# h and u in the weights' column order, and three q pairs turned by VectorE from quarter rows

## The chip, the cores and the metric

The kernel runs on one core of a Trainium2 chip. Five engines work at the same time, each through its own queue in order: TensorE (PE, with its weight loads shown apart as PEld), VectorE (DVE), ScalarE (ACT), GpSimd (POOL) and SyncE (SP). DMA transfers are issued from the queues of SP, ACT and POOL. The metric is the time of one execution on the device in microseconds (us); lower is better.

## What is computed

One layer of attention over a sparse graph, with a layer norm before it and a residual behind it. There are N = 2708 nodes with D = 1024 features, all float32. A row of `adj` has about four ones.

```python
h = jnp.maximum(_layernorm(x, axis=-1), 0.0)
q = h @ W_q.T + b_q
k = h @ W_k.T + b_k
v = h @ W_v.T + b_v
z = scale * (q @ k.T) * adj
z = jnp.where(z == 0.0, -10000.0, z)
attn = jax.nn.softmax(z, axis=1)
out = x + jax.nn.relu(attn @ v)
```

## The kernel before

**The algebra.** The kernel doesn't form k and v. It forms M = scale * W_q^T W_k once, then for each node the row q = h M + b, the scores z as products of q with the rows h of the node's neighbours, u as the softmax-weighted sum of those same rows, and the output as relu(u W_v + b_v) + x. The neighbours' rows are gathered from `h_dram` in HBM by indirect DMAs.

**Tiles.** The nodes are sorted by their number of neighbours into 22 tiles of 128 rows (the last one is small). A tile of rows lies in SBUF as 128 partitions of 1024 columns.

**The order of columns.** The weights come from HBM with their 1024 columns in the order "p c": feature c * 128 + p stands at column p * 8 + c. A slice of W_q for one c therefore takes every eighth column (`a_tile`, L464). Before the change h, q and u lie in natural order, "c p". The product that makes M comes out of PE in the weights' order, so `evicted` (L489) and `joined` (L492) permute its columns while they copy it from PSUM to SBUF, and so does the copy of the bias at L596.

**Units.** From about 106 us on, the work of PE is a sequence of 20 units, each a pair of tiles: ten q pairs (tiles 0 to 19) and ten o pairs (u times W_v). A unit multiplies 256 rows by a 1024x1024 matrix in seven block products instead of eight, with sums and differences of blocks (`multiply`, L1044, `opened`, L1015, `add_block`, L1008). Each block product is eight records of PE of 128x512, written to the banks `ps` or `psy`. The right-hand blocks are M and T (T is built by `ts_of_m`, L438, and lies in `wlow`).

**Turning the rows.** The left-hand blocks need features on the partitions, so each pair of tiles has to be turned. `blocks` (L711) makes, for a pair (xa, xb), the turned halves a11, a12 (of xa), a22 and a21 (of xb), and from these s1 = a22 + a21, s3 = a11 - a21, s2 = s1 - a11 and s4 = a12 - s2. There are two ways of turning. In `half_turned` (L410) PE turns 128x128 squares against an identity: the square is PE's stationary operand, four turns go into one PSUM bank, and ScalarE copies the bank to SBUF (L718). The q pairs go this way, and two single u tiles that are kept in SBUF. In `faces` (L703) VectorE turns 32x32 squares with one instruction for half a tile (L705); that only gives the wanted result if the rows were laid out by quarters first, and `by_quarters` (L695) does that with four DMAs from SP when u is read back from `u_dram`. For that, ScalarE first copies u into a tile v with the columns of a quarter side by side (L944) and stores v. The o pairs go this way.

**Where the rows of a q pair come from.** Units 0 to 3 (tiles 0 to 7) use the tiles that the layer norm left in SBUF. Units 4 to 9 gather their rows of h from HBM on POOL (`load_rows`, L1198, `gather`, L607) once the table of sorted rows is back in SBUF.

**What sets the order.** In unit n the function `after(i)` (L1245) runs between the products: it asks for the turning of pair n + 1 (upper half at i = 0, lower half at i = 2, in a few units later), for the rows of pair n + 2, and advances the stream of scores (L863) and sums (L923) on VectorE by an amount of work for each step. ScalarE and VectorE follow a fixed order up to unit 4, VectorE up to the end; POOL follows one up to unit 2 and is then ordered by the scheduler. Before the units, `stats`, `root`, `apply` (L270) and `keep` (L278) make h: `apply` writes relu of the normed x over x. POOL adds each tile into `hsum` (L285, L298). The positions `pos_i` for the sort of tiles 0 to 7 are made at (3, 6), that is unit 3, step 6; POOL then scatters the table (`put`, L622, written at L626), it is loaded back, and the gathers for the scores (L610) begin.

## Time and profile before

| what | value |
|---|---|
| median of 3 runs | 635.86 us (634.95 to 635.87) |
| the profiled execution | 631.83 us |
| its span in the profile | 630.1 us |
| instructions | 6067 |
| DMA moved | 182.19 MB |

The profile shows one execution. Its stages are: products of the weights up to about 104 us; q units from 106 to about 350 us; o units up to about 605 us; a single last tile up to 624 us. In a row of the profile, L1010 is line 1010 of the kernel, `out<-in,in` gives tiles by the program's names, `x8` is a count, and what stands in brackets is idle time of the engine before the row with what ended it. A group's row ends in busy us, mean ns of one, and idle us before. Records of PE overlap, because a product is still draining when the next one begins; the distance between starts is what one costs.

The kernel's line that a row names is one before the change. Of the rows used below, L415 is a turn on PE, L476 a product of the weights, L1010 a product of a unit, L705 a half turn on VectorE, L722 the making of s1 to s4, L863 a score, L923 a sum.

### The profile page before, as it was taken

The page shows a single profiled execution, that of the slowest core. Times are in us where ns is not written, and L with a number is a line of the kernel's source. Part 1 is how long each engine was busy: PE and PEld are TensorE (multiplying, and loading weights), DVE is VectorE, ACT ScalarE, POOL GpSimd, SP SyncE. Part 2 cuts the span into 40 slices and gives each one's busy share as a digit, 9 for nine tenths or more (in the row PEclk, how much of TensorE's full clock was granted, in tenths as well). Part 3 has the DMA queues.
Part 4 walks back from the last instruction along what each step waited for, and adds up shares of the span by engine and source line. Part 5 has one row for each costly group of instructions (what it writes and reads, how often), then busy time and mean ns, then how long its engine had stood idle before and what let it go on. Part 6 is the DMA issues. An engine that isn't in the chain of part 4 may idle for free.

```text
span 630.1 us, 6067 instructions
## 1 busy us (share of the span) xinstructions
PE 619.6 (98%) x1579; PEld 310.3 (49%) x1579; DVE 523.3 (83%) x1022; ACT 288.4 (46%) x421; POOL 363.1 (58%) x394
## 2 busy tenths in 40 slices
PE   8999999999999999999999998999999999999996
PEld 5777766444444444454454443444444444444442
DVE  5999879997996664887988969999997999988741
ACT  3538985749677563343341333434342323343300
POOL 2649860885778177754561632757667477852241
PEclk9999999999999999999999999999999999999999
DMA  8999997688796439997489998899999999997481
GB/s 330 407 371 326 343 354 294 209 288 326 255 387 241 166 113 319 350 379 236 154 306 325 332 359 265 235 333 346 347 318 324 344 278 305 349 284 194 103 296 71
DMA packets 65088, 182.19 MB, mean 289 GB/s; under 512 B 9959, under 2 KB 20023, under 8 KB 64408
## 3 DMA queue, kind: packets, MB, share of 16 engines
q0 software_dynamic: 26656, 86.02, 43.4%
q1 hardware_dynamic: 31594, 71.53, 32.8%
q10 hardware_dynamic: 6798, 24.20, 9.8%
q8 instruction: 14, 0.23, 0.2%
q14 instruction: 26, 0.21, 0.1%
HBM read 146.70 MB, written 43.36 MB: 302 GB/s over the span
## 4 chain that ended last, share of the span: by engine, by line
PE 56%; DMA 17%; DVE 11%; issue 9%; POOL 4%; ACT 1%; SPq 1%; POOLq 0%; DVEq 0%; ACTq 0%
PE ps L1010 22%; PE psy L1010 15%; PE ps_y L476 7%; DMA out_dram<-y,tab 5%; PE ps_x L476 4%; DMA or<-u_dram 4%; PE ps_z L476 4%; DVE junk L863 4%; PE pt L415 3%; DMA pq<-q_late 2%; DVE u L923 2%; DMA q_late<-q 2%; DMA g<-h_dram,tab 2%; DMA u_dram<-v 1%; DVE a L705 1%
## 5 line engine op out<-in xcount | busy, mean ns | idle before, releaser
L1010 PE MATMUL psy<-wlow,s 128*128 128x512 f32 x320 | 144.0, 592 | 0.0
L1010 PE MATMUL ps<-M,a 128*128 128x512 f32 x320 | 144.0, 593 | 0.0
L610 POOL DMA_INDIRECT g<-h_dram,tab x91 | 110.3, 1212 | 55.8 <-ACT u L912 19.8
L863 DVE SCALAR_TENSOR_TENSOR junk<-g,pq 128x1024 uint8<-128x1024 f32 x90 | 110.0, 1223 | 16.8 <-DMA g<-h_dram,tab 10.2
L1010 PE MATMUL ps<-M,s 128*128 128x512 f32 x240 | 108.0, 592 | 2.2 <-DVE s L722 2.2
L1010 PEld LDWEIGHTS psy<-wlow,s 128*128 128x128 f32 x320 | 59.9, 190 | 72.4 <-issue 70.2
L1010 PEld LDWEIGHTS ps<-M,a 128*128 128x128 f32 x320 | 59.9, 190 | 71.8 <-issue 71.3
L923 DVE SCALAR_TENSOR_TENSOR u<-g,coef,u 128x1024 f32<-128x1024 f32 x66 | 84.6, 1282 | 4.9 <-ACT u L912 3.5
L1010 PEld LDWEIGHTS ps<-M,s 128*128 128x128 f32 x240 | 45.4, 190 | 59.7 <-issue 58.3
L389 DVE FIND_INDEX8 at<-ones,adj 128x8 uint32<-128x685 f32 (+1 forms) x88 | 74.5, 865 | 0.0
L1010 PE MATMUL psy<-wlow,a 128*128 128x512 f32 x160 | 72.0, 593 | 0.1
L368 ACT ACTIVATE sized<-adj 128x2708 uint8<-128x2708 f32 (+1 forms) x22 | 54.3, 2466 | 7.5 <-DMA adj<-in_adj_dram 6.1
L298 POOL TENSOR_TENSOR hsum<-hsum,x 128x256 f32<-128x256 f32 (+1 forms) x56 | 38.7, 728 | 25.4 <-DVE wlow L444 22.0
L1109 POOL DMA_INDIRECT y<-in_x_dram,tab x19 | 32.2, 1696 | 31.4 <-ACT y L1126 22.4
L1010 PEld LDWEIGHTS psy<-wlow,a 128*128 128x128 f32 x160 | 30.3, 190 | 38.7 <-issue 37.3
L944 ACT COPY v<-u 128x1024 f32<-128x1024 f32 x19 | 19.9, 1045 | 48.9 <-DVE u L923 43.5
L808 POOL DMA_INDIRECT out_dram<-y,tab x21 | 27.8, 1325 | 22.0 <-issue 13.6
L1010 PE MATMUL ps<-wlow,s 128*128 128x512 f32 x80 | 36.0, 592 | 0.0
L626 POOL DMA_INDIRECT tab_dram<-tab,pos_i x22 | 21.9, 993 | 20.9 <-DVE pos_i L689 15.4
L912 ACT ACTIVATE u<-g,coef 128x1024 f32<-128x1024 f32 x18 | 20.7, 1148 | 24.2 <-DVE coef L911 24.1
L760 ACT COPY ps<-bp_sb 128x512 f32<-128x512 f32 x42 | 24.6, 595 | 11.0 <-DVE y L1144 10.3
L276 ACT ACTIVATE x<-x,r 128x1024 f32<-128x1024 f32 (+1 forms) x22 | 25.8, 1232 | 5.6 <-POOL r L266 5.6
(251 smaller groups left out, 848.5 us busy)
## 6 DMA issues: line engine op xcount, KB each, us to landing
adj<-in_adj_dram SPq DMA_DIRECT2D x21, 1354.0 KB, 11.2
x<-in_x_dram SPq DMA_DIRECT2D x21, 512.0 KB, 4.2
h_dram<-x ACTq DMA_DIRECT2D x21, 512.0 KB, 8.4
u_dram<-v ACTq DMA_DIRECT2D x19, 512.0 KB, 8.5
or<-u_dram SPq DMA_DIRECT2D x76, 128.0 KB, 9.7
q_late<-q SPq DMA_DIRECT2D x12, 512.0 KB, 9.4
pq<-q_late POOLq DMA_DIRECT2D x12, 512.0 KB, 10.5
M<-in_wv_dram SPq DMA_DIRECT2D x3, 1024.0 KB, 15.4
```

The lines of the kernel that those rows point to most:

```text
L276: nc.scalar.activation(xs[i][:n], xs[i][:n], AF.Relu, bias=r[:n, 4, i:i + 1], scale=r[:n, 3, i:i + 1])
L298: small.append(nc.gpsimd.tensor_add(hsum[:n, cols], hsum[:n, cols], xt[:n, cols]))
L368: nc.scalar.activation(sized[:n], a[:n, :, :PW], AF.Abs, accum_out=total[:n, t:t + 1])
L389: nc.vector.max_index(at[:n, k - first_k, g, :], ones[:n, 0:8], a[:n, g, :])
L476: mm = nc.tensor.matmul(bank, a_tile(o + H * a[0], a[1], i), b(o), start=first and o == 0, stop=(o == H - 1), skip_group_check=True)
L610: return nc.gpsimd.indirect_dma_start(out=dst, out_offset=None, in_=src, in_offset=off, bounds_check=N - 1, oob_is_err=False)
L760: nc.scalar.copy(return_[h], row[:, h * NB:(h + 1) * NB])
L808: to = nc.gpsimd.indirect_dma_start(out=out, out_offset=bass.IndirectOffsetOnAxis(ap=ptab.bitcast(U32)[:n, t, SLOTS:SLOTS + 1], axis=0), i ...
L863: chained(lambda: nc.vector.scalar_tensor_tensor(junk, g_of[t][s], 1.0, tq[t], op0=ALU.mult, op1=ALU.mult, accum_out=zall[:, t, s:s + 1]))
L923: chained(lambda: nc.vector.scalar_tensor_tensor(u, g_of[t][s], coef[:, s:s + 1], u, op0=ALU.mult, op1=ALU.add))
L1010: mm = nc.tensor.matmul(bank, a[:, c, :], b[:, c, :], start=False, stop=(c == 3), skip_group_check=True)
L1109: return nc.gpsimd.indirect_dma_start(out=y[:n], out_offset=None, in_=x, in_offset=off, compute_op=ALU.add)
```

## The change

h, q, M and u now lie in the weights' column order "p c" everywhere, and three q pairs are turned by VectorE.

- `evicted`, `joined` and the copy of the bias no longer permute; `joined` is one instruction for a bank instead of two. `ts_of_m` works on contiguous halves and its order is slightly different.
- `apply` writes h into another tile than x, with the columns permuted: each write steps over eight columns (32 bytes). For this there is one more row tile (`row_extra`), and the seven row tiles are now handed out by name.
- A turn on PE takes every eighth column of the tile as its square (`half_turned`), in place of 128 neighbouring columns.
- `faces` reads every eighth column of the laid-out tile, in place of runs of 32 neighbours.
- u is stored as it is; the copy v on ScalarE is gone.
- The q pairs of units 5, 6 and 7 (tiles 10 to 15) are gathered by quarter rows: `quarter_ids` makes an index table with 16 small operations on VectorE, and `gather_quarters` issues four indirect DMAs for a tile, 256 columns each, in place of one of 1024. These tiles go through `faces`.

```diff
     def apply(first, only=range(4)):
...
-                nc.scalar.activation(xs[i][:n], xs[i][:n], AF.Relu, bias=r[:n, 4, i:i + 1], scale=r[:n, 3, i:i + 1])
+                ht = spare.pop()
+                nc.scalar.activation(ht[:n].rearrange("p (m c) -> p c m", c=DC), xs[i][:n].rearrange("p (c m) -> p c m", c=DC),
+                                     AF.Relu, bias=r[:n, 4, i:i + 1], scale=r[:n, 3, i:i + 1])
+                spare.append(xs[i])
...
     def half_turned(xt, s):
...
-            k = s * 4 + c
-            nc.tensor.transpose(pt[:, c, :], xt[:, k * P:(k + 1) * P], ident)
+            nc.tensor.transpose(pt[:, c, :], xt.rearrange("p (m c) -> p c m", c=DC)[:, s * 4 + c], ident)
...
         def joined(bank, g, half, i):
-            for j in range(2):
-                nc.vector.scalar_tensor_tensor(place(g, half, i)[:, j], taken(bank)[:, j], scale,
-                                               place(g, half, i)[:, j], op0=ALU.mult, op1=ALU.add)
+            nc.vector.scalar_tensor_tensor(place(g, half, i), bank, scale, place(g, half, i), op0=ALU.mult, op1=ALU.add)
...
+    quartered = range(2 * FIRST + 2, 2 * FIRST + 8)
...
+        for g in range(QUADS):
+            for a in range(QUADS):
+                nc.vector.tensor_scalar(quarter_i[a * QP:(a + 1) * QP, g], ptab.bitcast(U32)[g * QP:(g + 1) * QP, lo:hi, SLOTS],
+                                        float(QUADS), float(a), op0=ALU.mult, op1=ALU.add)
+
+    def gather_quarters(dst, t):
+
+        faced.append(dst)
+        for g in range(QUADS):
+            off = bass.IndirectOffsetOnAxis(ap=quarter_i[:, g, t - quartered[0]:t - quartered[0] + 1], axis=0)
+            nc.gpsimd.indirect_dma_start(out=dst[:, g * D // QUADS:(g + 1) * D // QUADS], out_offset=None,
+                                         in_=h_dram.rearrange("n (a j) -> (n a) j", a=QUADS), in_offset=off)
...
         return nc.vector.transpose(dst.rearrange("p c (g r) -> p g c r", r=QP),
-                                   xt.rearrange("p (g c r) -> p g c r", g=QUADS, r=QP)[:, :, lo:hi])
+                                   xt.rearrange("p (g r c) -> p g c r", g=QUADS, r=QP)[:, :, lo:hi])
...
-            v = row_tile(f"v_{t}")
-            nc.scalar.copy(v.rearrange("p (a c r) -> p c a r", a=QUADS, r=QP),
-                           u.rearrange("p (c a r) -> p c a r", a=QUADS, r=QP))
-            nc.scalar.dma_start(u_dram[t * P:(t + 1) * P, :], v)
+            nc.scalar.dma_start(u_dram[t * P:(t + 1) * P, :], u)
...
-            if kind == "q":
+            if kind == "q" and t in quartered:
+                gather_quarters(rows[-1], t)
+            elif kind == "q":
                 gather(rows[-1], h_dram[:, :], t, SLOTS, P)
...
-                rows_of[FIRST + 1] = load_rows(units[FIRST + 1])
                 pooled.close()
+            if (n, i) == (3, 0):
+                quarter_ids()
+                rows_of[FIRST + 1] = load_rows(units[FIRST + 1])
```

On PE, in unit 4, between the product of a22 and that of s2 and further, the rows before are these (`qr` are the gathered rows of tiles 10 and 11, `pt` the bank of turned squares; a row with x8 is eight turns, one of x4 a block product):

```order
L1010 MATMUL psy<-wlow,a_1236 128x512 x4
L678 LDWEIGHTS before
L678 MATMUL ps_in<-sort,before 128x144
L680 LDWEIGHTS ones_h
L680 MATMUL ps_all<-sort,ones_h 128x144
L415 MATMUL pt<-ident,qr_1312 128x128 x8
L1010 MATMUL psy<-wlow,s_1434 128x512 x4
L415 MATMUL pt<-ident,qr_1314 128x128 x8
L1010 MATMUL ps_1373<-M,a_1396 128x512 x4
```

And now:

```order
L1026 MATMUL psy<-wlow,a_1220 128x512 x4
L698 LDWEIGHTS before
L698 MATMUL ps_in<-sort,before 128x144
L700 LDWEIGHTS ones_h
L700 MATMUL ps_all<-sort,ones_h 128x144
L1026 MATMUL psy<-wlow,s_1436 128x512 x4
L1026 MATMUL ps_1375<-M,a_1398 128x512 x4
```

The two rows of eight turns are gone; the same holds for the next two units.

On VectorE, in unit 5, where the first scores and the s blocks of unit 6 are made (`g` are gathered rows, `pq` the rows of q, `junk` the product that is thrown away), the rows before are:

```order
L863 SCALAR_TENSOR_TENSOR junk_1673,zall<-g_1402,pq_1611 128x1024
L863 SCALAR_TENSOR_TENSOR junk_1675,zall<-g_1403,pq_1611 128x1024
L863 SCALAR_TENSOR_TENSOR junk_1677,zall<-g_1404,pq_1611 128x1024
L722 TENSOR_TENSOR s_1691<-a_1684,pt 128x512
L722 TENSOR_TENSOR s_1693<-a_1658,pt 128x512
L722 TENSOR_TENSOR s_1695<-s_1691,a_1658 128x512
```

And now:

```order
L723 STREAM_TRANSPOSE a_1640<-row_168 128x4x4x32
L723 STREAM_TRANSPOSE a_1642<-row_168 128x4x4x32
L882 SCALAR_TENSOR_TENSOR junk_1650,zall<-g_1404,pq_1598 128x1024
L882 SCALAR_TENSOR_TENSOR junk_1652,zall<-g_1405,pq_1598 128x1024
L882 SCALAR_TENSOR_TENSOR junk_1654,zall<-g_1406,pq_1598 128x1024
L723 STREAM_TRANSPOSE a_1656<-row_169 128x4x4x32
L723 STREAM_TRANSPOSE s_1658<-row_169 128x4x4x32
L740 TENSOR_TENSOR s_1660<-a_1656,s_1658 128x512
```

Four half turns have come in, two ahead of the scores and two behind them, and s1 no longer reads a bank of PE.

On POOL, between the last additions to `hsum` and the scatter of the early table, the rows before are (`qr` again gathered rows, of tiles 10 to 13):

```order
L298 TENSOR_TENSOR hsum<-hsum,x_945 128x256 x4
L612 DMA qr_1312<-h_dram,tab 128x1024
L612 DMA qr_1314<-h_dram,tab 128x1024
L612 DMA qr_1579<-h_dram,tab 128x1024
L612 DMA qr_1581<-h_dram,tab 128x1024
L626 DMA tab_dram_70<-tab,pos_i 1024x18 x8
```

And now, with `row` for the row tiles of tiles 10 to 15:

```order
L310 TENSOR_TENSOR hsum<-hsum,row_167 128x256 x4
L634 DMA row_166<-h_dram,quarter_i 128x256 x4
L634 DMA row_167<-h_dram,quarter_i 128x256 x4
L634 DMA row_168<-h_dram,quarter_i 128x256 x4
L634 DMA row_169<-h_dram,quarter_i 128x256 x4
L634 DMA row_164<-h_dram,quarter_i 128x256 x4
L634 DMA row_165<-h_dram,quarter_i 128x256 x4
L646 DMA tab_dram_70<-tab,pos_i 1024x18 x8
```

24 indirect DMAs of 256 columns stand ahead of the scatter, where four of 1024 columns stood.

More of the change, by code (lines that the diff above doesn't have):

```diff
@@ L438, in ts_of_m @@
     def ts_of_m(part, *which):
-        cut = slice(part * (P // NH), (part + 1) * (P // NH))
-        m = [[M[:, i, j].rearrange("p c (b w) -> p (c b) w", w=P)[:, :, cut] for j in range(2)] for i in range(2)]
-        t = [T[:, k].rearrange("p c (b w) -> p (c b) w", w=P)[:, :, cut] for k in range(4)]
+        cut = slice(2 * part, 2 * part + 2)
+        m = [[M[:, i, j, cut] for j in range(2)] for i in range(2)]
+        t = [T[:, k, cut] for k in range(4)]
         for k in which:
```

59 lines of the change are left out of this document (30 added, 29 removed).

## Prediction

> **What bounds the kernel now.** I read the page first, for the busy shares, and then who waited for whom on PE.
>
> ```profile
> span 630.1 us, 6067 instructions
> PE 619.6 (98%) x1579; PEld 310.3 (49%) x1579; DVE 523.3 (83%) x1022; ACT 288.4 (46%) x421; POOL 363.1 (58%) x394
> ```
>
> ```profile
> PE ps L1010 <- DVE s L722: 2.2, 1, 2.2
> PE ps_y L511 <- POOL hsum L121: 1.2, 1, 1.2
> PE ps L1010 <- DVE T_alone L705: 0.8, 1, 0.8
> PE ps_x L476 <- DMA wlow<-in_wq_dram: 0.6, 1, 0.6
> ```
>
> PE is busy for 619.6 of 630.1 us, and all its waits add to 4.8 us. A busy PE need not be PE at its best, so I looked at the stretches: the columns are PE, PEld, DVE, ACT and POOL busy with counts, then granted clock, DMA share and GB/s.
>
> ```profile
> 35.00:107.00 72.00, 72.00 (x187) 52.38 (x187) 63.98 (x161) 52.79 (x65) 43.78 (x63) 1.00 0.92 339
> 107.00:200.00 93.00, 93.00 (x250) 43.38 (x249) 82.50 (x213) 67.56 (x82) 66.61 (x103) 1.00 0.81 290
> ...
> 240.00:330.00 90.00, 90.00 (x259) 43.39 (x258) 74.62 (x120) 33.57 (x57) 56.41 (x49) 1.00 0.84 290
> 330.00:400.00 70.00, 67.84 (x159) 29.79 (x158) 62.63 (x104) 22.75 (x37) 25.16 (x22) 1.00 0.95 305
> 400.00:600.00 200.00, 200.00 (x479) 89.30 (x478) 181.56 (x294) 73.34 (x119) 124.24 (x95) 1.00 0.95 294
> ```
>
> PE is full in every stretch shown but one, at the full granted clock of 1.00. **So each microsecond that PE's own queue gains or loses comes out at the end**, unless VectorE, 0.9 busy from 330 us on, is late instead. The chain of waits shows what the turns cost PE now:
>
> ```profile
> 138.74 0.87 PE pt L415 x8
> ```
>
> Eight turns of 128x128 take 0.87 us, 0.109 us each.
>
> **Part 1: turns taken from PE.** Three pairs leave PE, 16 turns each, 48 of the 176 that the table below counts (64, 96 and 16): 48 x 0.109 = **-5.2 us**. ScalarE loses nine copies of 0.59 us with them, and the 19 copies of u; both lie beside PE.
>
> **Part 2: the turns that stay.** 176 - 48 = 128 stay on PE. Their stationary operand was a block of 128 neighbouring columns and is now every eighth column, a step of 32 bytes. The trace has that step already: the products of the weights (L476) load wq's columns with the same step of eight. The rows of the weight load, with its mean in ns after the comma:
>
> ```profile
> L1010 PEld LDWEIGHTS ps<-M,a 128*128 128x128 f32 x320 | 59.9, 190 | 71.8 <-issue 71.3 <-ACT ps L760 0.5
> ...
> L415 PEld LDWEIGHTS pt<-ident,qr 128*128 128x128 f32 x96 | 11.2, 141 | 5.8 <-issue 5.6 <-DVE g L1262 0.2
> ...
> L476 PEld LDWEIGHTS ps_x<-wk,wq 128*128 128x128 f32 x32 | 10.0, 313 | 3.7
> ...
> L415 PEld LDWEIGHTS pt<-ident,x 128*128 128x128 f32 x64 | 7.4, 141 | 3.3 <-issue 3.2
> L415 PEld LDWEIGHTS pt<-ident,u 128*128 128x128 f32 x16 | 1.9, 141 | 1.1 <-issue 1.1
> ...
> L594 PEld LDWEIGHTS ps_v<-acc_b,ones 128*128 128x128 f32 x4 | 0.8, 190 | 0.8 <-issue 0.5 <-PE ps_y L476 0.2
> ```
>
> The same 128x128 f32 load is 190 ns with neighbouring columns, 313 with the step; L594 stands among the L476 loads in time and is 190, so the step makes the difference, not the stage. Today those 313 ns are hidden, since one L476 product takes 13.9 us / 32 = 0.43 us. A turn has only 0.109 us to hide a load. How close two loads can follow each other is seen where nothing covers them, right after a wait of PE:
>
> ```profile
> 5.70 0.55 PEld L476 LDWEIGHTS ps_x<-wlow 128*128 128x128 f32 x2 [1.04 <-DMA wlow<-in_wk_dram]
> ...
> 390.41 0.30 PEld L1010 LDWEIGHTS ps<-M,s 128*128 128x128 f32 x2 [2.96 <-issue]
> ...
> L476 PE MATMUL ps_x<-wk,wq 128*128 128x512 f32 x32 | 13.9, 592 | 0.0
> ```
>
> Two loads with the step take 0.55 us together, so the second starts 0.55 - 0.31 = 0.24 us after the first; without it 0.30 - 0.19 = 0.11. The part of a record that holds up the next load is thus its length less 0.08: 0.11 of 0.19, 0.23 of 0.31, 0.06 of 0.14. No row shows a turn with the step. Its load is bounded below by 0.06 (then nothing changes, the 0.109 of the turn covers it) and above by 0.24. I take 0.232, the nearest row: the same tile, type and step. The first load of a run hides under the product before it; in PE's order the 128 turns stand in 15 runs (one of 16, fourteen of 8), so 113 are uncovered: 113 x (0.232 - 0.109) = **+13.9 us**, with ends 0 and 113 x 0.131 = +14.8.
>
> [...]
>
> **Part 3: VectorE.** It gets 12 half turns of the three pairs, and all its half turns now read with the step of 32 bytes.
>
> ```profile
> L705 DVE STREAM_TRANSPOSE a<-or 128x512 f32<-128x512 f32 x28 | 18.6, 693 | 0.0
> ...
> L688 DVE TENSOR_REDUCE deg<-sort 128x14 f32<-128x252 f32 x1 | 0.6, 594 | 0.0
> L688 DVE TENSOR_REDUCE deg<-sort 128x8 f32<-128x144 f32 x1 | 0.4, 420 | 0.0
> L662 DVE TENSOR_REDUCE bad<-sort 128x14 f32<-128x224 f32 x1 | 0.4, 386 | 0.0
> L662 DVE TENSOR_REDUCE bad<-sort 128x8 f32<-128x128 f32 x1 | 0.3, 285 | 0.0
> ```
>
> A half turn is 0.69 us. L688 reads its 144 elements with just this step, its 252 with 56 bytes; L662 reads neighbours. Per element that is (594 - 420) / 108 = 1.61 ns against (386 - 285) / 96 = 1.05. I take 512 x 0.56 ns, **about +0.3 us for a half turn**, ends 0 and +0.4 (by 420 against 302 at 144 elements). Where it counts is where products wait for VectorE:
>
> ```profile
> 379.88 1.30 DVE L705 STREAM_TRANSPOSE a<-or 128x512 f32<-128x512 f32 x2
> ...
> 388.90 0.66 DVE L705 STREAM_TRANSPOSE s<-or 128x512 f32<-128x512 f32 x1
> 389.60 0.69 DVE L722 TENSOR_TENSOR s<-a,s 128x512 f32<-128x512 f32 x1
> ...
> 390.44 3.67 PE L1010 MATMUL ps<-M,s 128*128 128x512 f32 x8 [2.16 <-DVE s L722]
> ...
> 411.97 0.69 DVE L722 TENSOR_TENSOR s<-a,s 128x512 f32<-128x512 f32 x1
> ...
> 414.55 1.88 PE L1010 MATMUL ps<-M,s 128*128 128x512 f32 x4
> ```
>
> At 390 us PE already waits 2.16 for s1, and four half turns stand ahead of it from 379.88 on: 4 x 0.3 = **+1.3 us** with rounding up. At 414 s1 is 1.9 us early and the next four are covered. The other 28 from 400 us on add 9 us, less than the 18.4 us that VectorE is idle there.
>
> The quarter gathers meet VectorE through POOL, whose queue they enter ahead of the tables' scatter:
>
> ```profile
> 206.59 0.93 POOL L612 DMA_INDIRECT qr<-h_dram,tab  x1 [0.30 <-issue]
> 219.24 1.00 POOL L626 DMA_INDIRECT tab_dram<-tab,pos_i  x1 [11.72 <-DVE pos_i L689]
> ...
> 240.75 1.23 DVE L863 SCALAR_TENSOR_TENSOR junk<-g,pq 128x1024 uint8<-128x1024 f32 x1 [5.17 <-DMA g<-h_dram,tab]
> ...
> 248.05 1.28 DVE L722 TENSOR_TENSOR s<-a,pt 128x512 f32<-128x512 f32 x2 [3.21 <-ACT a L718]
> ...
> 260.98 3.60 PE L1010 MATMUL ps<-wlow,s 128*128 128x512 f32 x8
> ```
>
> A gather takes 0.93 us and 0.30 to the next; 24 stand there instead of 4, so 20 x 1.23 = 25 us, of which POOL's 11.72 of idle time take half. The scatter, and with it the first scores on VectorE, comes about 13 us later if PE is not delayed, and some 10 if it is (part 2 holds up the sort too). Behind those scores stands s1 of unit 6, made at 248.7 and needed at 260.98: 12.2 us of slack, and the wait of 3.21 for ScalarE's copies goes while two half turns of 1.0 come. That just covers it. VectorE must then win back its lag, up to 13.3 - 3.2 + 2.0 + 4.0 (unit 7) + 1.2 = 17.3 us, by 390 us; it has 15.4 - 5.2 - 3.2 = 7.0 idle us to 330 and 7.4 to 400, 14.4. If all of the lag comes, 2.9 us reach PE; with the 1.3 that is +4.2. The other end is -2.2, the wait at 390 gone. I keep +1.3.
>
> **Part 4: hidden.** ScalarE's 22 writes of h now step 32 bytes.
>
> ```profile
> L276 ACT ACTIVATE x<-x,r 128x1024 f32<-128x1024 f32 x21 | 24.7, 1232 | 5.6 <-POOL r L266 5.6
> ...
> L944 ACT COPY v<-u 128x1024 f32<-128x1024 f32 x19 | 19.9, 1045 | 48.9 <-DVE u L923 43.5 <-DVE u L929 5.3
> ```
>
> Even at VectorE's price for such reads (1024 x 0.82 ns) these are 18 us, in the 45 us that ScalarE is idle between 35 and 200 us; without that cover they would hold up evictions one for one. The 16 index operations lie in VectorE's 10.5 idle us before 200. Evictions without a permutation and eight joins for sixteen gain nothing, as PE waits for none of them. At the end, u's copy of 1.05 us leaves the way to T_alone and the double half turn gains 0.6: zero, within the 0.8 that PE waits there.
>
> **Sum.** -5.2 + 13.9 + 1.3 = **+10.0 us**. The profiled execution took 631.83 us (span 630.1), the runs' median is 635.86. I add the sum to the median: **645.9 us**. Its own range runs from -5.2 + 13.9 - 2.2 = +6.5 to -5.2 + 14.8 + 4.2 = +13.8: 642.4 to 649.7.
>
> **The rivals.**
> - *The step is hidden on PE: faster.* If a turn's load passes each element once where a product's passes it twice, which 0.06 against 0.11 would allow, the step makes 0.06 x 2.14 = 0.126 at most, 113 x 0.017 = +1.9 us. Then -5.2 to -3.3, about 631.6. Place: the runs of eight turns. It decides at a load of 0.144 us: below it (5.2 - 1.3) / 113 = 0.035 a turn is not used up. For it: nothing shows a turn paying. [...] Against it: 0.24 us for the same read.
> - *The step adds its 0.123 to the 0.06.* Then a load is 0.182: 113 x 0.073 = +8.2, in sum +4.3, 640.2.
> - *The step is hidden, and VectorE becomes the bound.* The lag of part 3 in full: -5.2 to -3.3, and +4.2, in the middle about 635.8, no change. For it: the 2.16 at 390.
>
> **How the numbers follow.** A measurement of this kernel can tell about 0.2%, 1.3 us. Chances: the forecast 0.50, the added step 0.13 (both slower: 0.63), VectorE as the bound 0.13 (same), the hidden step 0.24 (faster). The range of 631.5 to 649.7 leaves out the better half of the faster case and the forecast's worst.
>
> **What would show it.** Eight turns take 0.87 us in the chain if the step is free, 0.98 if hidden up to 0.126, 1.7 by the forecast; a turn's load is 0.31 long, not 0.14; half turns on VectorE are near 1.0 us; POOL's first scatter of the early table starts with no idle time before it; PE's wait for s1 near 390 us is over 3. It is wrong if the load of a turn stays under 0.15 us, or if a new wait of PE between 250 and 400 us is larger than 4.2.

## The result, and the profile after

The changed kernel takes **669.1 us** (667.91 to 670.36, four runs); the kernel before, on the same chip beside it, 635.87 us. The ratio is 1.0522, with a 95% interval from 1.0494 to 1.0551: slower by 33.2 us. The forecast was +10.0 us and its range ended at 649.7.

The head of the page of the changed kernel, beside 630.1 us, 98% PE and 523.3 us of DVE before:

```profile
span 668.3 us, 5994 instructions
...
PE 625.4 (94%) x1531; PEld 309.2 (46%) x1531; DVE 551.9 (83%) x1042; ACT 287.5 (43%) x393; POOL 382.2 (57%) x412
```

TensorE has 48 matmuls less and was still busy 5.8 us longer; its idle time went from 10.5 to 42.9 us. The waits of PE say for what (engine, tile and line waited for, then us in total, times, longest):

```profile
PE psy L1026 <- issue: 13.2, 1, 13.2
PE pt L426 <- ACT M L496: 5.7, 2, 5.3
PE psy L1026 <- DVE q L1107: 4.9, 2, 3.4
PE psy L1026 <- ACT psy L1039: 2.9, 2, 2.5
PE ps L1026 <- ACT ps L778: 2.7, 1, 2.7
PE ps L1026 <- DVE T_alone L723: 2.6, 1, 2.6
PE ps L1026 <- DVE s L740: 1.9, 1, 1.9
```

Before, the longest wait was 2.2 us. Now TensorE waits for copies on ScalarE (the evictions of L496 and L1039, and L778, which puts the bias into a bank), for VectorE (q, s, T_alone), and once for something that the profile does not show ("issue"). The stretches, with the columns of those before:

```profile
35.00:107.00 72.00, 68.79 (x161) 49.31 (x159) 58.59 (x130) 60.86 (x52) 44.61 (x62) 1.00 0.85 314
107.00:200.00 93.00, 89.20 (x252) 44.24 (x252) 80.89 (x222) 71.70 (x81) 59.15 (x92) 0.96 0.76 267
240.00:330.00 90.00, 74.86 (x181) 33.70 (x182) 61.63 (x100) 25.24 (x44) 58.31 (x62) 0.92 0.72 242
330.00:400.00 70.00, 66.49 (x163) 29.64 (x162) 65.14 (x99) 19.90 (x34) 34.92 (x28) 0.98 0.89 292
400.00:600.00 200.00, 198.07 (x471) 87.79 (x470) 191.69 (x292) 61.97 (x108) 121.46 (x96) 1.00 0.98 302
```

Every stretch has lost some of TensorE's time, the last one 1.9 us, and in the three between 107 and 400 us the granted clock is under 1.00 too. Where the time went is seen best by setting the same product of the two kernels side by side. Both run the same 140 block products on TensorE and then the last tile; the table gives how much later a product starts in the changed kernel than in the kernel before, at the places where that changes most (the two profiled executions; starts in us). Smaller steps are left out, four of about 0.67 us between 442 and 529 us among them:

```
before   after    later by  step
106.58   114.74    8.16    +8.16   first products of the blocks
190.37   201.19   10.82    +2.71
217.15   227.23   10.08    -0.87   eight turns gone; so at 221, 243, 247, 269 and 273
228.33   250.95   22.62   +13.37   the wait "issue"
231.76   256.19   24.43    +1.81   a product of 5.2 us instead of 3.4
235.19   262.45   27.26    +2.83
290.20   315.74   25.54    +1.68
367.52   397.54   30.02    +3.59   waits for q on VectorE
370.95   402.78   31.82    +1.80
390.44   419.94   29.50    -2.32   the wait of 2.16 before is gone
584.79   619.06   34.26    +2.06   waits for s on VectorE
588.23   624.26   36.03    +1.77
610.11   648.51   38.41    +2.37   waits for T_alone on VectorE
```

The profile of the kernel before was taken at 631.83 us, 4 us under its median, and that of the changed kernel at 670.0, 0.9 us above, so the end of this table stands some 5 us above the difference of the medians. What the three edits cost an instruction, from the groups by form (before: 1.23 us for the write of h, 0.69 for the half turn, 0.93 for a gather):

```profile
L283 ACT ACTIVATE row<-row,r 128x1024 f32<-128x1024 f32 x12 | 27.2, 2264 | 0.3
...
L723 DVE STREAM_TRANSPOSE a<-row 128x512 f32<-128x512 f32 x37 | 39.2, 1086 | 0.0
...
L634 POOL DMA_INDIRECT row<-h_dram,quarter_i x24 | 23.1, 962 | 7.2 <-issue 7.2
```

And the turns that stayed on PE, by their weight loads (min/median/max in ns) and in PE's order of time:

```profile
L426 PEld LDWEIGHTS pt<-ident,row x120: 186/189/230, 109.1 to 579.0; 128*128 128x128 f32 x120
```

```profile
146.64 1.05 PE L426 MATMUL pt<-ident,row 128*128 128x128 f32 x8
147.53 3.60 PE L1026 MATMUL psy<-wlow,s 128*128 128x512 f32 x8
```

The product starts 0.89 us after the first of eight turns; before it was 0.87. The rows of eight turns ahead of a product take 0.87 to 0.89 us each, under 0.2 us more in all. The +13.9 us on TensorE, on which the forecast rested, is not there; nearly everything lost was lost in parts 3 and 4, where the forecast had 1.3.

### The profile page after: what moved, and what is told of

The parts are those of the page before. It is cut to its first block, busy times and chain, and to the rows that moved or that the text cites. A ratio compares the mean times of both kernels' runs of the same rounds, so it can differ in the third digit from the quotient of the medians.

```text
span 668.3 us, 5994 instructions
## 1 busy us (share of the span) xinstructions
PE 625.4 (94%) x1531; PEld 309.2 (46%) x1531; DVE 551.9 (83%) x1042; ACT 287.5 (43%) x393; POOL 382.2 (57%) x412
## 4 chain that ended last, share of the span: by engine, by line
DVE 24%; issue 21%; DMA 19%; PE 17%; ACT 10%; POOL 6%; SPq 1%; ACTq 1%; POOLq 0%; DVEq 0%
PE ps L1026 9%; DMA g<-h_dram,tab 7%; PE psy L1026 6%; DVE row L942 6%; DVE junk L882 5%; DMA u_dram<-row 4%; ACT row L283 3%; POOL g L612 2%; DVE a L723 2%; DMA out_dram<-y,tab 2%; DMA row<-u_dram 2%; ACT x L283 2%; DVE s L740 2%; DVE acc_b L536 2%; DMA adj<-in_adj_dram 1%
## 5 line engine op out<-in xcount | busy, mean ns | idle before, releaser
L1026 PE MATMUL psy<-wlow,s 128*128 128x512 f32 x320 | 146.2, 600 | 17.2 <-issue 13.2
L612 POOL DMA_INDIRECT g<-h_dram,tab x91 | 112.0, 1230 | 59.4 <-DVE row L942 20.1
L942 DVE SCALAR_TENSOR_TENSOR row<-g,coef,row 128x1024 f32<-128x1024 f32 x66 | 84.4, 1279 | 3.8 <-ACT row L931 2.4
L1026 PE MATMUL psy<-wlow,a 128*128 128x512 f32 x160 | 74.2, 607 | 6.1 <-DVE q L1107 4.9
L723 DVE STREAM_TRANSPOSE a<-row 128x512 f32<-128x512 f32 x37 | 39.2, 1086 | 0.0
L931 ACT ACTIVATE row<-g,coef 128x1024 f32<-128x1024 f32 x18 | 20.7, 1149 | 37.1 <-DVE coef L930 25.9
L310 POOL TENSOR_TENSOR hsum<-hsum,row 128x256 f32<-128x256 f32 x44 | 30.4, 725 | 7.5 <-ACT row L283 3.4
L778 ACT COPY ps<-bp_sb 128x512 f32<-128x512 f32 x42 | 24.5, 592 | 20.1 <-DVE y L1160 12.8
L827 POOL DMA_INDIRECT out_dram<-y,tab x20 | 25.5, 1274 | 11.6 <-issue 4.9
L891 ACT ACTIVATE w<-zall 128x3 f32<-128x3 f32 (+6 forms) x20 | 4.1, 207 | 57.7 <-DVE junk L882 57.7
L487 PE MATMUL ps_y<-wlow 128*128 128x512 f32 x64 | 27.6, 592 | 0.0
```

What stands on the lines that cost most here:

```text
L310: small.append(nc.gpsimd.tensor_add(hsum[:n, cols], hsum[:n, cols], xt[:n, cols]))
L487: mm = nc.tensor.matmul(bank, a_tile(o + H * a[0], a[1], i), b(o), start=first and o == 0, stop=(o == H - 1), skip_group_check=True)
L612: return nc.gpsimd.indirect_dma_start(out=dst, out_offset=None, in_=src, in_offset=off, bounds_check=N - 1, oob_is_err=False)
L723: return nc.vector.transpose(dst.rearrange("p c (g r) -> p g c r", r=QP), xt.rearrange("p (g r c) -> p g c r", g=QUADS, r=QP)[:, :, lo:hi])
L827: to = nc.gpsimd.indirect_dma_start(out=out, out_offset=bass.IndirectOffsetOnAxis(ap=ptab.bitcast(U32)[:n, t, SLOTS:SLOTS + 1], axis=0), i ...
L942: chained(lambda: nc.vector.scalar_tensor_tensor(u, g_of[t][s], coef[:, s:s + 1], u, op0=ALU.mult, op1=ALU.add))
```

## The experiments

**The kernel again, and three parts undone one by one.** All four beside the same runs of the kernel before (636.35 us). A name in brackets is the run's, by which the text calls it later. Where an expectation speaks of late signals, it means copies that ScalarE starts microseconds after the product that they copy has ended, with nothing in the trace for which they waited. First the changed kernel unchanged (again):

> The changed kernel once more, unedited. Its first profile has 13.2 us of idle TensorE at 237.7 us, ended by nothing that the profile shows, while ScalarE's copy of psy waits 18.6 us for a TensorE product that had ended. If that stall belongs to the program (whatever causes it), the second profile has it at the same product, within 1 us, and the time is again 667 to 671 us. If it is an accident of one execution, the gap is gone or stands at another product and the span moves by some 10 us.

671.12 us, +34.8 (ratio 1.0532, 1.0436 to 1.0629). The result stands, and its profile has the wait without a releaser at the same product, now of 14.7 us.

*ScalarE writes h with neighbouring columns (plain_write):*

```diff
-  nc.scalar.activation(ht[:n].rearrange("p (m c) -> p c m", c=DC), xs[i][:n].rearrange("p (c m) -> p c m", c=DC),
+  nc.scalar.activation(ht[:n], xs[i][:n],
```

> The changed kernel, with relu of x written in the natural order (ScalarE's output contiguous; h then has the wrong column order, everything else runs as before). Theory A, ScalarE's price: one application takes 2.26 us with the 32-byte step and 1.23 us without, 22 of them add 22.7 us to ScalarE's queue, and this alone makes the TensorE waits at 104 us (5.3 us for M's eviction, 8.2 us with the slow turns behind it) and at 199 us (2.7 us): both go, and the time falls by 10 to 11 us to about 658. If the 13.2 us at 238 us also hang on a late ScalarE, it falls by 25 to 29 us, to 640 to 644. Theory B, the quarter gathers on GpSimd carry it: the gaps at 104 and 199 us may go, but the wait at 238 us stays or grows, and the time stays over 655. If ScalarE's price were hidden, as the forecast had it: no change, 668.

665.61 us, +29.3 (1.0446, 1.0352 to 1.0539). The write is back at 1.24 us, and TensorE is not late any more at the first products (8.2 us late in the changed kernel, 0.1 early here) nor at 195 us; yet only 5.5 us of that reach the end. By 310 us this kernel is 23.7 us behind: the waits in the middle take most of it back.

*The three pairs gathered whole, 6 DMAs for 24 (whole_rows):*

```diff
-                gather_quarters(rows[-1], t)
+                gather(rows[-1], h_dram[:, :], t, SLOTS, P), faced.append(rows[-1])
```

> The changed kernel, with the three pairs' rows gathered whole (6 gathers in the place of 24; the rows then arrive unpermuted, so their turns are wrong in content, and are still made by VectorE). GpSimd's queue loses 18 issues of 1.25 us ahead of the table's scatter, which moves from 245.6 to about 228 us. Theory B: the waits at 238 us (13.2 us, with 1.8 us of lower clock) and 260 us (2.7 us) go, and the time falls by 13 to 18 us to 651 to 656. Theory A (a late ScalarE or VectorE makes the wait at 238 us): no change within 3 us.

654.89 us, +18.5 (1.0278, 1.0186 to 1.0370): 16.2 us for 18 gathers. The wait without a releaser is gone, and at 310 us TensorE is 10.6 us behind instead of 26.

*Half turns on VectorE that read runs of 32 neighbours (faces_plain):*

```diff
-   xt.rearrange("p (g r c) -> p g c r", g=QUADS, r=QP)[:, :, lo:hi])
+   xt.rearrange("p (g c r) -> p g c r", g=QUADS, r=QP)[:, :, lo:hi])
```

> The changed kernel, with VectorE's half turns reading runs of 32 elements, as before, in the place of steps of 32 bytes (content wrong). One half turn falls from 1.09 to 0.69 us, 48 of them 18.7 us of VectorE. Theory C, VectorE's price decides the lag after 300 us (1.7 us near 290 us, 5.4 us at 368, 3.8 us at 585, 2.4 us at the last tile): it falls by 6 to 12 us, to 657 to 663. Theories A and B alone: within 3 us of 669.

659.10 us, +22.8 (1.0344, 1.0251 to 1.0436): 12.0 us. From 400 us on the changed kernel loses 9.0 us against the kernel before; this one gains 1.4, and the waits for q near 390, for s near 617 and for T_alone are not in its profile.

Alone, the three give back 5.5, 16.2 and 12.0 us, some 34 together. **All three at once (three_plain):**

> The changed kernel with the three edits at once: relu of x written in the natural order, whole rows gathered, half turns reading runs of 32 (content wrong in all three; queues and order as in the changed kernel, 18 gathers fewer). If ScalarE's price, the quarter gathers and VectorE's price are all that the change costs, each counts by itself: 671 less 11 (waits at 104 and 199 us), less 16 (whole_rows), less 12 (faces_plain), 630 to 634, under the 636 of before by the 5.2 us of the 48 turns. If something else costs too (the 128 turns left on TensorE, the copies of v moved), it stays over 637.

632.53 us beside 635.64, ten runs: -3.1 (0.9959, 0.9943 to 0.9975). The group of half turns on VectorE in this kernel, by form:

```profile
L723 DVE STREAM_TRANSPOSE a<-row 128x512 f32<-128x512 f32 x37 | 24.6, 691 | 0.0
```

So the three hold 34.8 + 3.1 = 37.9 us (each difference is taken beside its own runs of the kernel before), and what is left of the change loses nothing. It bounds what this layout could give if its three prices were nothing: about 3 us.

**How the gathers cost.** No pair (no_quarters), or one pair (one_pair), by quarters; the other q pairs turned by PE, in the new column order:

```diff
-            if kind == "q" and t in quartered:
+            if kind == "q" and t in ():
```

> The changed kernel, with the three q pairs gathered whole and turned by TensorE, as the others (content right). The 48 turns come back for 5.2 us; 18 gathers and 12 half turns go. Theory B (the quarter gathers make the waits at 238 and 260 us): 655 (whole_rows) plus 5 less up to 3 for VectorE's 12 half turns, 656 to 661, no TensorE signal over 5 us late after 220 us. If the late signals come from the half turns or the layout: the wait at 238 us stays, 670 or more.

```diff
-            if kind == "q" and t in quartered:
+            if kind == "q" and t in quartered[:2]:
```

> The changed kernel, with only the first of the three pairs gathered by quarters (8 gathers, 10 us of GpSimd, ahead of the table's scatter). If the wait at 238 us grows with the number of gathers, about a third of its 13 to 18 us stays, 4 to 6 us; if it needs a long row of them (signals are still on time for the first 10 us of the gathers in the changed kernel), nothing stays, and the time is that of no_quarters less 1.7 us.

654.33 us, +18.7 (1.0291, 1.0245 to 1.0336), and 657.20 us, +21.6 (1.0336, 1.0296 to 1.0376), both beside 635.64. One pair saves TensorE 16 turns, 1.7 us, and the kernel is 2.9 us slower, though the two intervals overlap; its profile has the wait without a releaser again, of 6.2 us, where no_quarters has none. And no_quarters settles part 2: it runs 32 turns between the products at 243 and 273 us with the step, and its lag behind the kernel before stays at 12.1 to 12.2 us, at 227, 260, 289 and 310. A turn with the step costs TensorE next to nothing there.

**A step in the read instead of the write (strided_read):**

```diff
-  activation(ht[:n].rearrange("p (m c) -> p c m", c=DC), xs[i][:n].rearrange("p (c m) -> p c m", c=DC),
+  activation(ht[:n].rearrange("p (m c) -> p m c", c=DC), xs[i][:n].rearrange("p (c m) -> p m c", c=DC),
```

> The changed kernel, with the same h (content right), but ScalarE writes it contiguously and reads x with a step of 512 bytes in the place of writing with a step of 32 bytes. If only the write is dear, one application takes 1.23 us and the time is that of plain_write, 665 to 667; if the read's step costs as much, 2.26 us and 669 to 672; in between it costs by the step.

669.07 us, +33.4 (1.0523, 1.0482 to 1.0563): no better. ScalarE's group in this kernel:

```profile
L283 ACT ACTIVATE row<-row,r 128x1024 f32<-128x1024 f32 x12 | 26.3, 2194 | 0.3
```

**The gathers alone, in the kernel before (before_quartered):** its tiles 10 to 15 fetched by quarters, everything else as it was.

```diff
+            if kind == "q" and 10 <= t < 16:
+                if t == 10:
+                    for a in range(QUADS):
+                        nc.vector.tensor_scalar(quarter_i[:, a], ptab.bitcast(U32)[:, 10:16, SLOTS],
+                                                float(QUADS), float(a), op0=ALU.mult, op1=ALU.add)
+                for a in range(QUADS):
+                    off = bass.IndirectOffsetOnAxis(ap=quarter_i[:, a, t - 10:t - 9], axis=0)
+                    nc.gpsimd.indirect_dma_start(out=rows[-1][:, a * D // QUADS:(a + 1) * D // QUADS], out_offset=None,
+                                                 in_=h_dram.rearrange("n (a j) -> (n a) j", a=QUADS), in_offset=off)
```

> The kernel before, in its own column order, with the rows of the tiles 10 to 15 gathered by four gathers of 1 KB columns each in the place of one of 4 KB (the same content; 18 gathers and 4 small index operations more; 16 of the 24 stand ahead of the table's scatter; the turns stay on TensorE). If the quarter gathers alone make TensorE's signals late, ScalarE starts 5 to 20 us after a product's end near 225 to 255 us, TensorE stands idle there for 6 to 15 us, and the time is 643 to 655. If it takes the changed order of the columns, VectorE's half turns or the fixed row tiles too: at most the scatter's delay of some 10 us is felt, behind 12 us of slack, 635 to 639, and no signal is over 3 us late.

640.63 us beside 632.98: +7.7 (1.0118, 1.0088 to 1.0149). The waits of PE that are new are for the quarters themselves and for s:

```profile
PE pt L415 <- DMA qr<-h_dram,quarter_i: 3.7, 3, 2.7
PE ps L1011 <- DVE s L723: 2.6, 1, 2.6
```

So without any other part the gathers cost more than the 5.2 us that the whole change takes from TensorE. It is a milder case than the changed kernel: 16 of the 24 gathers stand ahead of the scatter, which starts at 223.49 us beside 219.24.

**Two of the three pairs gathered behind the early table's scatter (quarters_late):**

```diff
-            nc.gpsimd.indirect_dma_start(out=dst[:, g * D // QUADS:(g + 1) * D // QUADS], out_offset=None,
...
+            with tc.issue_after(puts[0][-1].ins) if t >= quartered[2] else nullcontext():
+                nc.gpsimd.indirect_dma_start(out=dst[:, g * D // QUADS:(g + 1) * D // QUADS], out_offset=None,
...
```

> The changed kernel, with the quarter gathers of the last two of the three pairs issued behind the table's scatter (8 ahead of it, 8 ahead of the first score gathers, 8 among them; the same content). If the wait at 238 us comes from a long unbroken row of gathers ahead of the scatter, it falls to the 6 us of one_pair or less, and the time to 657 to 662, or lower by the turns that are saved. If every quarter gather delays signals wherever it stands, waits turn up at the moved ones too, and the sum of the waits between 220 and 320 us stays at 13 us or more, 665 to 672.

665.07 us, +32.1 (1.0504, 1.0474 to 1.0535), beside 632.98. The scatter is earlier (its last DMA is issued at 237 us, in the changed kernel at 254.5), and the lag at 274 us falls to 8.8, but at 310 us it is 21.6: now 8 of the moved gathers stand between the scatter and the rows g of the first scores, the other 8 between these and later rows g, and TensorE waits 4.5 us for u, 1.9 for s and 4.1 for q. Moving the gathers in POOL's queue moves the wait; it does not take it away.

**The same on another occasion.** The wait of 13.2 us in the profiled run has a releaser that the trace doesn't show, so both kernels and two experiments were measured anew (before_again, again_2, whole_rows_2, before_quartered_2).

> The kernel before, unedited. If late signals belong to the occasion, its trace shows them too whenever the other three do (ScalarE's copies 1 to 4 us after a product's end near 170 to 185 us), and it then takes 635 to 637 us; where signals are on time, 632 to 634. If they belong to the changed kernel, this trace shows none in either case.

> The changed kernel, unedited, for the third time. If late signals belong to the kernel, the wait of 13 to 18 us near 238 us is there again and the time is 667 to 672. If they belong to the occasion and this one has none, that wait shrinks to what GpSimd's long queue makes by itself, and the time is 655 to 664.

> The changed kernel with whole rows gathered, for the second time: 652 to 655 us with signals late or on time, since the first run showed them late by 2 us only. The difference to again_2 is what the quarter gathers cost: 14 to 18 us with late signals, and if it is under 8 us without them, the late signals are more than half of that price.

> The kernel before with the quarter gathers, for the second time. On an occasion without late signals 638 to 642 us, 7 us over before as in the first run. On one with late signals, if the quarter gathers alone bring them on, a TensorE wait of 6 to 20 us near 230 to 255 us and 646 to 660; if they take the changed kernel, 638 to 642 again.

The kernel before against itself: 1.0032 (1.0008 to 1.0055), so 0.3% is what two kernels can differ by for nothing, and the 0.4% of three_plain is little more. The others beside 632.47 us: 667.01, +34.5 (1.0533, 1.0476 to 1.0591); 653.14, +20.7 (1.0314, 1.0263 to 1.0366); 642.22, +9.8 (1.0142, 1.0054 to 1.0230). The changed kernel loses the same, and here its profile has no wait of TensorE without a releaser. Its largest waits of PE are

```profile
PE psy L1026 <- ACT u L1070: 10.9, 4, 9.6
PE psy L1026 <- DVE q L1107: 8.0, 2, 5.8
PE pt L426 <- ACT M L496: 5.1, 2, 4.7
```

and the path of the first can be read in the order of time, in us from the start, with the idle time ahead of an instruction and what ended it in brackets:

```profile
241.89 0.95 POOL L634 DMA_INDIRECT row<-h_dram,quarter_i  x1 [0.31 <-issue]
243.14 1.00 POOL L646 DMA_INDIRECT tab_dram<-tab,pos_i  x1 [0.30 <-DVE g L1282]
256.91 0.23 DVE L972 TENSOR_SCALAR keys<-tab 128x128 f32<-128x128 uint32 x1 [13.98 <-DMA tab<-tab_dram]
264.46 1.23 DVE L882 SCALAR_TENSOR_TENSOR junk<-g,pq 128x1024 uint8<-128x1024 f32 x1 [5.24 <-DMA g<-h_dram,tab]
268.31 0.20 ACT L891 ACTIVATE w<-zall 128x3 f32<-128x3 f32 x1 [17.92 <-DVE junk L882]
268.42 0.57 ACT L1070 COPY u<-psy 128x512 f32<-128x512 f32 x1
269.04 2.93 PE L1026 MATMUL psy<-wlow,s 128*128 128x512 f32 x3 [9.60 <-ACT u L1070]
```

POOL's last quarter gather ends, the scatter follows at once; the table is there some 14 us later, its rows 7.5 us after that, and VectorE makes three scores. ScalarE has been standing for 17.92 us at the small operation on those scores, and the copy that frees TensorE's bank stands behind it in its queue. TensorE's product could have started up to 9.60 us earlier. In the kernel before the same operation came in time for TensorE:

```profile
244.87 0.20 ACT L872 ACTIVATE w<-zall 128x3 f32<-128x3 f32 x1 [5.46 <-DVE junk L863]
```

The profile of quarters_late has the same order on ScalarE, and behind it the 4.5 us that TensorE waits for u there:

```profile
262.18 0.20 ACT L892 ACTIVATE w<-zall 128x3 f32<-128x3 f32 x1 [12.78 <-DVE junk L883]
262.29 0.57 ACT L1071 COPY u<-psy 128x512 f32<-128x512 f32 x1
262.91 2.04 PE L1027 MATMUL psy<-wlow,s 128*128 128x512 f32 x3 [4.46 <-ACT u L1071]
```

**A test of that path (later_scores):** the first scores taken four steps later, so that evictions stand ahead of them.

```diff
-            if n > FIRST + 1 or n == FIRST + 1 and i > 1:
+            if n > FIRST + 1 or n == FIRST + 1 and i > 5:
```

> The changed kernel, with the stream of scores and sums started four steps of the unit later (the condition i > 1 is i > 5; same work, same content): ScalarE's first weights then stand behind the copies of psy, the two evictions and the next unit's copies, in the place of ahead of them. If the place on ScalarE's queue makes the wait near 259 us (9.6 us and 2 us of lower clock in again_2), it goes, and the time falls by 6 to 12 us to 655 to 661, less whatever VectorE then has to make up later. If TensorE waits for the late scores by another way, the wait stays over 5 us and the time at 664 or more.

687.00 us beside 636.75, +50.3 (1.0792, 1.0692 to 1.0893). A miss that decides nothing: its profile again has the wait without a releaser, and from 528 us on TensorE falls another 22 us behind, in waits for copies on ScalarE and for s and T_alone on VectorE, whose stream of scores had started later.

```profile
PE psy L1026 <- issue: 15.5, 2, 15.4
```

**The gathers alone, in the changed kernel (quarters_only):** plain write and plain half turns together, 24 quarter gathers kept (the edits of plain_write and faces_plain).

> The changed kernel with ScalarE's write and VectorE's half turns both in runs (content wrong): of the three prices only the quarter gathers are left. three_plain took 632.5 with whole rows; whole_rows_2 against again_2 puts the quarter gathers at 13.9 us. If prices add: 644 to 648. If VectorE's cheaper half turns give the late scores room to catch up: 637 to 643.

And the two single removals once more, beside the same runs (plain_write_2, faces_plain_2):

> The changed kernel with relu of x written in the natural order, for the second time. ScalarE's price is 7 to 8.5 us in the ledger of again_2 (up to 160 us). If it adds to the rest: 658 to 661. If the chain over GpSimd, which does not start earlier by as much, takes it back as in the first run: 662 to 666.

> The changed kernel with half turns that read runs, for the second time. In again_2 TensorE falls behind by 21 us after 273 us, in three_plain by 3.5. If VectorE's 18.7 us are the reason: 649 to 655. If only what shows on TensorE's waits for VectorE (some 12 us) is due to them, as the first run had it: 655 to 659.

Beside 636.75 us: 651.60, +14.9 (1.0236, 1.0151 to 1.0321); 665.49, +28.7 (1.0454, 1.0357 to 1.0552); 662.41, +25.7 (1.0406, 1.0320 to 1.0492). The gathers with the two prices gone cost more than either expectation, 14.9 + 3.1 = 18.0 us over three_plain, about what they gave back alone. The changed kernel was not measured on this occasion; against the 34.5 of again_2 the half turns give back some 9 us (12.0 the first time; 662.41 lies above both ranges expected), the write again under 6.

## Why the prediction was right in sign, by luck, and wrong in size

**Part 1 (-5.2 us): right on TensorE's queue.** The table has six steps of -0.87, and three_plain is 3.4 us ahead of the kernel before at 274 us, with a wait of 1.8 us for a gathered row that the latter hasn't. How much of it reaches the end is less clear: 3.1 us by the medians, where 0.3% (2 us) can come from nothing.

**Part 2 (+13.9 us): the step that failed first.** The prediction took "the nearest row: the same tile, type and step", the product's load of 313 ns. A turn's load with the step is 189 ns, against 141 without. Rival 1 was near: by its sum a turn's load with the step holds up the next for 0.126 us at most. By the prediction's own estimate, a record less 0.08, this load holds up the next for 0.109 us, and the turn it hides under takes 0.109. No run shows whether the rival's reason holds ("if a turn's load passes each element once where a product's passes it twice"). But before the change a turn's load already took 141 ns beside 190 for a product's, and that said more about the turns than a row of the same tile and step but another kind of matmul. The prediction's marks disagreed here: eight turns at 0.87 us meant "free", a load over 0.15 the opposite; the first is the direct one. The load grew by 48 ns with the step, but eight turns still take 0.87 to 0.89 us. Only at 109 to 115 us, right behind a wait of 5.31 us, did most of 23 turns stand 213 ns apart; the granted clock was 0.50 there (window 109 to 113 us). plain_write, with the same step and no such wait, is 0.1 us early there.

With part 2 at nothing the forecast's other terms make -5.2 + 1.3 = -3.9 us, a faster kernel. That "slower" came true is therefore luck: the term that gave the sign was not there, and terms put at 1.3 and at nothing took its place. The miss is 33.2 + 3.9 = 37.1 us, about the 37.9 that the three removals hold: all of it lies in what parts 3 and 4 held to be covered.

**Part 4 ("hidden"): wrong.** The price was nearly right: 2.26 - 1.23 = 1.03 us for 22 writes, 22.7 us against at most 18. The cover was not. The 45 us of ScalarE's idle time between 35 and 200 us are not where the writes stand:

```profile
101.73 2.23 ACT L283 ACTIVATE row_extra<-row,r 128x1024 f32<-128x1024 f32 x1 [2.11 <-POOL r L272]
104.00 2.22 ACT L283 ACTIVATE row<-row,r 128x1024 f32<-128x1024 f32 x1
106.02 2.46 ACT L380 ACTIVATE sized<-adj 128x2708 uint8<-128x2708 f32 x1
108.38 0.18 ACT L380 ACTIVATION_READ_ACCUMULATOR sized<-adj 128x1 f32 x1
108.47 0.58 ACT L496 ACTIVATE M<-ps_y 128x512 f32<-128x512 f32 x1
```

```profile
109.10 1.12 PE L426 MATMUL pt<-ident,row 128*128 128x128 f32 x4 [5.31 <-ACT M L496]
```

Two long writes and another operation stand back to back ahead of the eviction of M, and TensorE waits 5.31 us for it. The prediction wrote what would happen "without that cover"; it summed idle time over 165 us instead of looking at the queue ahead of each eviction.

**Part 3, half turns: price right, cover wrong.** +0.39 us each (0.69 to 1.09), inside the ends of 0 and 0.4. "The other 28 from 400 us on add 9 us, less than the 18.4 us that VectorE is idle there": 28 x 0.39 = 10.9 us, and VectorE went from 181.6 to 191.7 us busy of the 200, without filling it. Yet removing the step gives 9 to 12 us. A sum of idle time again hid the places where a turn stands right ahead of what TensorE waits for, as here ahead of the s that ends its 1.90 us at 619:

```profile
616.11 1.10 DVE L723 STREAM_TRANSPOSE a<-row 128x512 f32<-128x512 f32 x1
617.13 1.05 DVE L723 STREAM_TRANSPOSE s<-row 128x512 f32<-128x512 f32 x1
618.22 0.69 DVE L740 TENSOR_TENSOR s<-a,s 128x512 f32<-128x512 f32 x1
```

T_alone is such a turn itself (2.01 us, 1.25 before). The wait for s1 near 390 went, as the low end of part 3 had it, and a wait of 3.42 us for q stands at 394; no turn stands in the ten us ahead of that q, where VectorE works with hardly a pause; yet it and the waits for s and T_alone are all gone in faces_plain.

**Part 3, quarter gathers: the largest term, and a path missed.** The gathers cost what was said, 1.25 us each from start to start, 30 us. The scatter came 26.4 us later (219.24 to 245.59), not "about 13". From the first of these gathers to the scatter it took 30.4 us instead of 16.4, 14.0 more, as foreseen; but the first gather itself started 12.3 us late; POOL had waited 5.50 us for rows of h to be stored. Before, in the changed kernel, and in plain_write:

```profile
202.86 0.95 POOL L612 DMA_INDIRECT qr<-h_dram,tab  x1 [0.16 <-issue]
```

```profile
204.43 1.08 POOL L614 DMA_INDIRECT row<-h_dram,tab  x1 [5.50 <-DMA h_dram<-row]
...
215.19 0.96 POOL L634 DMA_INDIRECT row<-h_dram,quarter_i  x1 [0.16 <-issue]
...
245.59 1.00 POOL L646 DMA_INDIRECT tab_dram<-tab,pos_i  x1 [0.30 <-issue]
```

```profile
208.22 0.97 POOL L634 DMA_INDIRECT row<-h_dram,quarter_i  x1 [0.16 <-issue]
```

So 7.0 of the 12.3 us go with ScalarE's step; the other 5.4 stay without it (three_plain has its first such gather at 208.59 too), and what makes them was not traced. TensorE itself was 9.2 us late by then, so against it the scatter came 17 us later, where s1 had 12.2 us of slack. In plain_write TensorE is on time to within 1.1 us and the scatter starts at 239.07: against TensorE it is no earlier, and TensorE's wait near 250 is 13.9 us, which fits that undoing the write alone gives back so little. And the prediction followed the scores to VectorE only. They also pass through ScalarE, where the copy u stands behind them: the 9.60 us of again_2 and the 4.5 of quarters_late. That this queue is the path is read from those two traces; the one experiment on it decided nothing. It is not the path of the 13.2 us in the profiled run, where ScalarE's first operation on scores comes at 273.53 us, long after that wait. But both waits belong to the gathers: in each of the ten profiles with all 24 ahead of the scatter TensorE has a wait of 9.6 to 18.4 us between 231 and 270 us; in one_pair it is 6.2; and in the two of whole rows, in no_quarters and in three_plain there is no wait over 0.3 us in that stretch. What they cost in all is measured: 13.9 to 16.2 us with whole rows instead, 18.0 with the other two prices gone, 7.7 to 9.8 in the milder case of the kernel before. The third rival, with +4.2, had the gathers as the source and a quarter of the price, but VectorE as the engine that TensorE waits for; at the large wait it is ScalarE.

**The mark that was named for a wrong forecast** ("a new wait of PE between 250 and 400 us larger than 4.2") came in again_2 at 259 to 269 us with 9.6; in the profiled run it came just ahead of that stretch, at 238 to 251 us with 13.2.

**What stays open:** what released the wait of 13.2 us in the first profile (below), and with it whether GpSimd's queue or the DMA traffic of the quarter rows holds things up there; no run separates the two. Open too is how the 34 us split when all three prices are in, since single removals overlap with each other and with waits that take their time back.

## What to carry to other kernels

An edit that is hidden by idle time is hidden only if the idle time stands between it and the next instruction that another engine waits for: read the order of the queue around each eviction, not the sum over a stage. Where an engine's queue mixes evictions with work on data from a long chain (gather, scatter, reload, score), a delay of that chain stops the evictions too (in again_2 ScalarE stood for 17.92 us, and TensorE for 9.60 behind it). Take a row from the same kind of instruction before one of the same tile and step, and before a layout change moves five microseconds from the bound engine, price its step on every engine that reads or writes the tile.

## What the hardware showed that was not expected

**The step of 32 bytes has a price on three engines.** ScalarE's write of 1024 fp32 goes from 1.23 to 2.26 us (a read with a step of 512 bytes: 2.19), VectorE's half turn from 0.69 to 1.09, TensorE's load for a turn from 0.141 to 0.189, the last hidden: eight turns still take 0.87 to 0.89 us.

**The granted clock falls after some short waits.** In the changed kernel, windows around the wait of 13.2 us and around one of 1.90 us (columns as above; the granted clock is third from the right):

```profile
237.00:251.00 14.00, 0.79 (x3) 0.05 (x1) 4.34 (x6) 0.69 (x2) 10.65 (x12) 0.63 0.26 75
251.00:255.00 4.00, 4.00 (x6) 1.75 (x7) 0.00 (x0) 3.24 (x6) 3.08 (x4) 0.57 0.07 9
619.00:623.00 4.00, 3.94 (x6) 1.66 (x7) 3.86 (x5) 0.00 (x0) 0.00 (x0) 0.58 0.01 2
```

```profile
250.95 5.40 PE L1026 MATMUL psy<-wlow,s 128*128 128x512 f32 x8 [13.21 <-issue]
256.19 3.60 PE L1026 MATMUL ps<-M,a 128*128 128x512 f32 x8
...
619.06 5.37 PE L1026 MATMUL ps<-M,s 128*128 128x512 f32 x8 [1.90 <-DVE s L740]
```

The next product starts 5.24 us later instead of 3.43: each such wait costs 1.8 us more than its length, the steps of +1.81, +1.80 and +1.77 in the table. The means of 0.57 and 0.58 mix two values: the window from 619.7 to 623 us alone reads 0.50, that from 254.5 to 256 us 1.00. A wait of 1.90 us was enough here, while the wait of 2.16 us near 388 in the kernel before had no such product behind it (3.67 us for its eight matmuls, at a granted clock of 1.00 from 390.4 to 394.1 us). The length of a wait alone doesn't decide it.

**A copy that starts long after its data.** In the first profile of the changed kernel:

```profile
250.31 0.59 ACT L1070 COPY u<-psy 128x512 f32<-128x512 f32 x1 [18.64 <-issue]
```

The product that it copies ended near 230.9 us, and nothing that the trace shows ended those 18.64 us; TensorE's 13.21 us stand behind it. In nine of the ten profiles with all 24 quarter gathers ahead of the scatter ScalarE stands 15 to 22 us before such a copy between 230 and 260 us, and TensorE behind it; in again_2 it does not, and the loss of the changed kernel against the kernel before was the same either way, 34.8 and 34.5 us. Without the quarter gathers only no_quarters has one, of 7.95 us near 268, for which TensorE does not wait. What holds up the copy was not found.
